# A decoder block's attention values as three float32r products of split operands, with the output sums' in-place multiplications issued directly behind their products

## The chip, the cores and the metric

The kernel runs on one core of a Trainium2 chip. The metric is device time in microseconds (us) of one execution of the whole program, taken several times on the chip; the median is compared. In the profile, PE is the matrix engine, PEld its weight loads, DVE the vector engine, ACT the scalar engine, POOL the GpSimd engine, SP the engine that issues the DMAs. L423 is line 423 of the kernel before.

## The reference, cut to what matters

The program is one decoder layer on x of shape (8, 128, 512): grouped-query attention with 4-bit weights, then cross attention, then a gated low-rank feed-forward, each followed by a layer norm. The change is inside the first part:

```python
q = apply_rope(dequant(x, qw_q)); k = apply_rope(dequant(x, qw_k)); v = dequant(x, qw_v)
scores = einsum('bhqd,bhkd->bhqk', q, k) / sqrt(HD)          # 32 query heads, 8 key heads, HD = 128
attn = softmax(where(causal, scores, min))
ctx = einsum('bhqk,bhkd->bhqd', attn, v)                     # the values product that is changed
x = layernorm(x + dequant_matmul(ctx, qw_o, scales_o))       # its sums over heads are rescaled in place
```

All data is float32. The kernel writes a float32 matrix product in one of two ways: as one matmul on float32 tiles (the trace shows it as two MATMUL records), or as a sum of matmuls on float32r tiles, each operand split into a high part and a low remainder (one record per matmul).

## The kernel before, in words

**Stages.** Up to about 70 us the first weights and inputs are loaded and split. From there to about 505 us runs the attention stage. It has 64 steps: 8 key-head groups g times 8 sequences b. Four steps share one half `hf` of the batch; a half is the unit for which projections are computed. After the steps, a fixed string `ATT_END` (L43) finishes the output sums beside key projections of the cross attention. Cross attention and feed-forward follow and are not touched.

**One step** (L760 to L824) walks the string `SEQUENCE = 'TpOpApOVpOpOp'` (L80). Each letter first calls `tick()`, which advances a slot counter and issues every instruction that was put off until that slot by `later(n, f)` (L242). The order on PE, DVE, ACT and POOL is exactly the order in which the Python code issues (a manual schedule); the order of the DMA issues on SP is left to the scheduler. The letters are:

- `T`, `attention_turn` (L411): four transposes of the softmaxed scores `p` into a PSUM tile `tr`, and a copy on ACT to `pt` (L417).
- `p`: some projection units of a coming half (`group`, L314). A unit is two matmuls (L317) and an evacuation, on ACT for the first of four (L323) and on DVE for the others (L327). After the fourth unit the tile is complete: a query or key tile is then rotated (`rope`, L345: two DMAs that swap halves, then `t`, `sw`, `q` or `k` on POOL, L350 to L352), and a value tile is transposed into `trv` and copied by ACT to `v` (L364).
- `A`, `attention_probs` (L380): scores `sc` of the step two ahead (L384), row minima on DVE (L389), four exponentials on ACT three slots later (L398), then a reciprocal `rden` on DVE (L404) and the normalisation of `p` on POOL (L405).
- `V`, `attention_values` (L420): the product `av` of `v` and `pt` (L423) and its split into `ch` on ACT (L186) and `cl` on DVE (L187).
- `O`, one part of `attention_out` (L442): two matmuls onto a sum `po` (L453) in one of two PSUM banks, `out0` and `out1`, which the parts use in turn. For the first three of four heads the sum is then multiplied in place by a ratio on ACT (L460); the last goes to `accT`, on ACT for g = 0 (L462) and on DVE otherwise (L466). The next part on the same bank waits for that multiplication.

**Delays.** `DELAYS` (L109) gives for each put-off instruction the number of slots, first value while step 0 is issued, second afterwards. `out` is 1 in both, so L460 is issued one letter after its product. There is an entry `pl` of 3 and 2 slots that nothing uses.

**Banks and buffers.** Six PSUM banks (`turn`, L131) rotate over `ps`, `tr`, `trv`, `sc` and `av`: a tile's bank is wanted again by the sixth tile after it. SBUF pool `att` holds `q`, `k`, `v`, `p`, `pt`, `ch`, `cl`, `wo`; pool `proj` holds the projections' tiles and `w0_kv` (L504), low parts of the first weights.

**The last six steps** have no more projections of their own; L777 to L786 open the cross attention's tiles, whose splits (`xwkh`, `ctxh`, `xwvh` on ACT, their low parts on POOL and DVE) run beside them.

Of the kernel before, what the change touches and what calls it, by code (L numbers as in the profile page):

```python
# [10 lines left out]
F32 = mybir.dt.float32  # L11
F32R = mybir.dt.float32r
# [3 lines left out]
ALU = mybir.AluOpType  # L16
# [3 lines left out]
P = 128  # L20
B, S, D = 8, 128, 512
N = B * S
KT = D // P
NH, NKV, HD = 32, 8, 128
REP = NH // NKV
# [10 lines left out]
HALF = 4  # L36
# [51 lines left out]
D_COS = 4  # L88
D_SIN = 10
D_Q = 10  # L90
D_OUT = 1
D_STAT = 3
D_POW = 3
D_APPLY = 8
# [6 lines left out]
S_COS = 3  # L101
S_SIN = 10
S_Q = 10
S_OUT = 1
S_W = 6
S_VT = 6
S_LOAD = 11
# [8 lines left out]
    "q": (S_Q, D_Q),  # L116
    "out": (S_OUT, D_OUT),
    "w": (S_W, D_W),
# [16 lines left out]
def f32(ap):  # L135
    return ap.bitcast(F32)
# [3 lines left out]
def decoder_kernel(ctx: ExitStack, tc: tile.TileContext, a: dict, out: bass.AP):  # L140
    nc = tc.nc
# [7 lines left out]
    def bank(tag, name, shape=(P, 512)):  # L149
        tag = tag if tag in psum["n"] else "turn"  # L150
        return psum["pool"].tile(list(shape), F32, tag=tag, name=name, bufs=psum["n"][tag])

    def pool(name, side="left", bufs=1):
        cm = tc.tile_pool(name=name, bufs=bufs, side=side)
        return cm, cm.__enter__()
# [29 lines left out]
    def split2(hi, lo, src, n=1):  # L185
        nc.scalar.copy(hi, src)  # L186
        later(n, lambda: nc.vector.tensor_tensor(lo, src, f32(hi), ALU.subtract))  # L187
# [49 lines left out]

    delayed, slot, starting, instance = [], [0], [True], {}  # L240

    def later(n, f, projects=False):  # L242

        if slot[0] == 0 or n == 0:
            return f()
        delayed.append((slot[0] + n, f, projects))

    def delay(name):

        return DELAYS[name][0 if starting[0] else 1]  # L250
# [21 lines left out]
    att_cm, att = pool("att")  # L272
    proj_cm, proj = pool("proj", "right")
# [79 lines left out]

        return projection(g, hf, w, j, x[:], rope)

    def values(g, hf, w, v):
        n = f"{g}_{hf}"
        x = proj.tile([P, HN], F32, tag="x", name=f"xv{n}", bufs=3)

        def turn():  # L360
            tr = bank("tr", f"trv{n}", (P, HALF, HD))
            for t in range(HALF):
                nc.tensor.transpose(tr[:, t, :], x[:, ts(t, S)], ident[:])
            nc.scalar.copy(v[:], tr[:])  # L364

        return projection(g, hf, w, REP + 1, x[:], lambda: later(delay("vt"), turn, True))

    def projections(g, hf, w):

        n = f"{g}_{hf}"  # L370
        q = att.tile([P, REP, HN], F32, tag="q", name=f"q{n}", bufs=2)
        k = att.tile([P, HN], F32, tag="k", name=f"k{n}", bufs=2)
        v = att.tile([P, HALF, HD], F32, tag="v", name=f"v{n}", bufs=2)
        units = roped(g, hf, w, REP, k[:], "k")
        for r in (REP - 1, *range(REP - 1)):
            units += roped(g, hf, w, r, q[:, r, :], "q")
        units += values(g, hf, w, v)
        return {"q": q, "k": k, "v": v}, units

    def attention_probs(g, b, t):  # L380
        j, n = b % HALF, f"{g}_{b}"
# [29 lines left out]
    def attention_turn(g, b, p):  # L411
        n = f"{g}_{b}"
        tr = bank("tr", f"tr{n}", (P, REP, S))
        for r in range(REP):
            nc.tensor.transpose(tr[:, r, :], p[:, r, :], ident[:])
        pt = att.tile([P, REP, S], F32, tag="pt", name=f"pt{n}", bufs=2)
        nc.scalar.copy(pt[:], tr[:])  # L417
        return pt

    def attention_values(g, b, t, pt):  # L420
        j, n = b % HALF, f"{g}_{b}"
        av = bank("av", f"av{n}", (P, REP, S))
        nc.tensor.matmul(av[:], t["v"][:, j, :], pt[:], start=True, stop=True)  # L423
        if j == 0:
            for m in "hl":
                t["c" + m] = att.tile([P, REP, HN], F32R, tag="c" + m, name=f"c{m}{n}", bufs=2)
        split2(t["ch"][:, :, ts(j, S)], t["cl"][:, :, ts(j, S)], av[:], delay("cl"))
# [14 lines left out]
    def attention_out(g, hf, t):  # L442

        sums, n = {}, len(OUT_LANES)

        def part(c, r):
            if r == 0:
                sums[c] = bank(OUT_LANES[c % n], f"po{g}_{hf}_{c}")  # L450
            ps = sums[c]
            for i, m in enumerate("hl"):
                nc.tensor.matmul(  # L453
                    ps[:], o_w[g][:, r, ts(c, P)], t["c" + m][:, r, :],
                    start=(r == 0 and i == 0), stop=(i == 1), skip_group_check=True,
                )
            sc = ratios[:, c, g * REP + r : g * REP + r + 1]
            to = accT[:, c, ts(hf, HN)]
            if r < REP - 1:
                later(delay("out"), lambda: nc.scalar.activation(ps[:], ps[:], AF.Copy, scale=sc))  # L460
            elif g == 0:
                later(delay("out"), lambda: nc.scalar.activation(to, ps[:], AF.Copy, scale=sc))  # L462
            else:
                later(
                    delay("out"),
                    lambda: nc.vector.scalar_tensor_tensor(to, ps[:], sc, to, ALU.mult, ALU.add),  # L466
                )

        return [lambda c=c, r=r: part(c, r) for c0 in range(0, KT, n) for r in range(REP) for c in range(c0, c0 + n)]
# [9 lines left out]
    def new_qkv(g):  # L479
        return proj.tile([P, KT, COLS], F32R, tag="w", name=f"w{g}", bufs=2)  # L480

    def new_o(g):
        return att.tile([P, REP, D], F32R, tag="wo", name=f"wo{g}", bufs=2)


    w, wo = new_qkv(0), new_o(0)
# [14 lines left out]


    w0_q = att.tile([P, REP, D], F32R, tag="ch", name="w0_q", bufs=2)
    w0_kv = proj.tile([P, KT, 2 * HD], F32R, name="w0_kv")  # L504

    def w0_low(j):
        return w0_q[:, :, ts(j, HD)] if j < REP else w0_kv[:, :, ts(j - REP, HD)]
# [219 lines left out]
    for i in range(2 * KT):  # L727
        units.pop(0)()
        tick()
        if i in W0_AT:  # L730
            n = W0_AT.index(i) + 2
# [5 lines left out]
    units, more = units + more[:AHEAD], more[AHEAD:]  # L737
    for i, u in enumerate(units, KT):
# [7 lines left out]
        if i in PROBS_AT:  # L746
            b = PROBS_AT.index(i)
# [3 lines left out]
    units = more  # L751
    assert len(units) <= RAMP + WINDOW[3]
    turned, outs = {}, []
    steps = NKV * B

    def at(s):
        g, b = divmod(s, B)
        return g, b, halves[s // HALF]

    for s in range(steps):  # L760
        g, b, t = at(s)
        if s == STARTING:
            starting[0] = False
        w = (s + LEAD) % HALF
        if w == 0:
            h = (s + LEAD) // HALF + 1
            if h < 2 * NKV:
                halves[h], units = half(h)
            else:
                units = []  # L770
        if s == 1:
            scale_ratios()
        if s == B:
            load_small()
# [24 lines left out]
        if b >= HALF and g + 1 < NKV:  # L799
            if b == HALF:  # L800
                o_w[g + 1] = new_o(g + 1)
            load_o(g + 1, o_w[g + 1], b - HALF)

        slots = SEQUENCE.count("p")
        done = 0
        for i, what in enumerate(SEQUENCE):
            tick()
            if what == "p":
                done += 1
                n = len(now) * done // slots - len(now) * (done - 1) // slots  # L810
                start = len(now) * (done - 1) // slots
                for u in now[start : start + n]:
                    u()
            elif what == "T":
                turned[s] = attention_turn(g, b, probs.pop(s))
            elif what == "A":
                if s + LEAD < steps:
                    probs[s + LEAD] = attention_probs(*at(s + LEAD))
            elif what == "V":
                attention_values(g, b, t, turned.pop(s))  # L820
            elif outs:
                outs.pop(0)()
        if b % HALF == HALF - 1:
            outs += attention_out(g, b // HALF, t)  # L824
# [52 lines left out]
    for t in range(B):  # L877
        n = VALUES_FIRST * (t + 1) // B - VALUES_FIRST * t // B
# [7 lines left out]
        tr = transposed(other_bank(f"tr_x1{t}", (P, KT, S)), t)  # L886
        hf, c = t // HALF, ts(t % HALF, S)
# [201 lines left out]
    for hf in range(2):  # L1089
        for m in range(KT):  # L1090
            n = fills.pop(0) if ready else 0
# [548 lines left out]
```

## Time and profile before

| | us |
|---|---|
| median of 3 runs (lowest to highest) | 707.55 (704.76 to 708.47) |
| the profiled execution | 709.09 |
| its span | 707.3 |
| busy in the span: PE / PEld / DVE / ACT / POOL | 653.6 / 486.1 / 498.4 / 487.8 / 461.3 |
| busy from 292 to 350 us (58 us, two halves): PE / DVE / ACT / POOL | 56.78 / 43.72 / 48.81 / 45.97 |
| busy from 467 to 505 us (38 us): PE / DVE / ACT / POOL | 32.40 / 16.11 / 32.11 / 19.14 |

The mean granted PE clock of the execution was 0.976 of full speed. An engine's busy time is the time in which it executed something; PE's records overlap, since the end of a matmul is modelled with the time that its result takes to come out, so PE's busy share is not its load. In a row of groups the columns are: line, engine, operation, tiles (out<-in), shapes, count, then total busy us and mean ns of one, then the engine's idle time just before these instructions and what ended most of it. In a timeline a row is start in us, duration in us, engine, line, operation, tiles, count, and in brackets the idle time before it with what ended it. The chain of waits is followed back from the last instruction, always to what released it; its rows are start, duration, engine, tile, line, count.

### The profile page before, as it was taken

Reading aid. Unit: us, or ns where it says so; the run is one execution under the profiler, and the core shown is the slowest. Engines: PE = TensorE matmul, PEld = TensorE weight load, DVE = VectorE, ACT = ScalarE, POOL = GpSimd, SP = SyncE. Lnnn points to the kernel's source line nnn. Section 1 sums busy time; section 2 is a strip of 40 time slices with the busy share of each in tenths; the row PEclk is TensorE's granted clock in tenths of the full one; section 3 lists DMA queues with packets and bytes.
Section 4 is the critical chain, followed back from the end, with each engine's and each line's share of the span. In section 5 each row is a group of like instructions: output and inputs, shape, how many; then the busy total and the mean of one; then the engine's idle time right before and its main releaser. Section 6 shows DMA issues by size and latency. Waiting matters only on the chain.

```text
span 707.3 us, 11358 instructions
## 1 busy us (share of the span) xinstructions
PE 653.6 (92%) x3476; PEld 486.1 (69%) x3476; DVE 498.4 (70%) x1291; ACT 487.8 (69%) x1211; POOL 461.3 (65%) x450
## 2 busy tenths in 40 slices
PE   6899999999999999999999999978999998479996
PEld 4687678777777767778777777746786765456652
DVE  4869667687777877778777786754366789975465
ACT  3567898987897888888889778888634455323433
POOL 3644977967869678696796977886014367356514
PEclk9999999999999999999999999999999999759998
DMA  8762531532443243244133332244001001100003
GB/s 289 203 183 65 135 98 35 137 97 46 105 120 76 60 135 90 56 117 110 34 85 82 67 102 66 57 164 178 0 1 31 1 1 51 43 1 1 2 0 119
DMA packets 31773, 57.34 MB, mean 81 GB/s; under 512 B 4831, under 2 KB 7135, under 8 KB 31714
## 3 DMA queue, kind: packets, MB, share of 16 engines
q1 hardware_dynamic: 31714, 56.64, 29.4%
q8 instruction: 27, 0.44, 0.3%
q14 instruction: 32, 0.26, 0.1%
HBM read 33.55 MB, written 2.10 MB: 50 GB/s over the span
## 4 chain that ended last, share of the span: by engine, by line
PE 27%; DVE 11%; ACT 7%; POOL 5%; issue 3%; DMA 1%; DVEq 0%; POOLq 0%; SPq 0%; ACTq 0%
PE po L453 4%; PE ps L317 3%; PE pf L1203 3%; PE pxk L692 3%; ACT p L398 3%; PE pxv L656 2%; DVE top L988 2%; PE pxq L692 2%; DVE part L327 2%; POOL sw L351 1%; DVE E L999 1%; PE sc L384 1%; PE pg L1190 1%; ACT po L460 1%; PE av L423 1%
## 5 line engine op out<-in xcount | busy, mean ns | idle before, releaser
L317 PE MATMUL ps<-xh,w 128*128 128x512 f32 x336 | 157.1, 467 | 0.0
L327 DVE SCALAR_TENSOR_TENSOR part<-ps,scales,part 128x512 f32<-128x512 f32 x168 | 125.5, 747 | 32.5 <-ACT part L323 15.0
L317 PE MATMUL ps<-xl,w 128*128 128x512 f32 x336 | 132.3, 394 | 0.0
L460 ACT ACTIVATE po<-po,ratios 128x512 f32<-128x512 f32 x192 | 123.9, 651 | 9.6 <-PE po L453 8.9
L453 PE MATMUL po<-ch,wo 128*128 128x512 f32 x256 | 115.5, 451 | 14.4 <-ACT po L460 13.8
L405 POOL TENSOR_TENSOR p<-p,rden 128x512 f32<-128x512 f32 x64 | 67.2, 1050 | 77.7 <-DVE rden L404 66.3
L398 ACT ACTIVATE p<-p,nmx 128x128 f32<-128x128 f32 x256 | 99.7, 392 | 16.7 <-DVE nmx L389 16.1
L453 PE MATMUL po<-cl,wo 128*128 128x512 f32 x256 | 101.2, 395 | 0.0
L351 POOL TENSOR_TENSOR sw<-sw,tables 128x512 f32<-128x512 f32 x71 | 91.9, 1294 | 13.6 <-DMA sw<-x 12.9
L352 POOL TENSOR_TENSOR q<-t,sw 128x512 f32<-128x512 f32 x62 | 81.5, 1315 | 15.5 <-DVE sw L351 11.1
L350 POOL TENSOR_TENSOR t<-x,tables 128x512 f32<-128x512 f32 x70 | 90.3, 1290 | 0.0
L453 PEld LDWEIGHTS po<-ch,wo 128*128 128x128 f32 x256 | 48.1, 188 | 46.4 <-ACT po L460 30.3
L317 PEld LDWEIGHTS ps<-xh,w 128*128 128x128 f32 x336 | 63.4, 189 | 19.1 <-DVE nmx L389 3.6
L317 PEld LDWEIGHTS ps<-xl,w 128*128 128x128 f32 x336 | 63.5, 189 | 18.6 <-issue 10.1
L389 DVE CUSTOM_DVE_ANT_0 p<-sc,causal 128x128 f32<-128x128 f32 x256 | 58.8, 286 | 23.2 <-PE sc L384 23.2
L384 PEld LDWEIGHTS sc<-k,q 128*128 128x128 f32 x512 | 68.0, 193 | 9.2 <-POOL q L352 2.6
L323 ACT ACTIVATE part<-ps,scales 128x512 f32<-128x512 f32 x84 | 58.0, 691 | 20.8 <-PE ps L317 20.8
L384 PE MATMUL sc<-k,q 128*128 128x128 f32 x512 | 69.4, 278 | 2.8 <-POOL q L352 2.0
L187 DVE TENSOR_TENSOR cl<-av,ch 128x512 fp32r<-128x512 f32 x64 | 44.2, 690 | 34.4 <-ACT ch L186 32.4
L327 DVE SCALAR_TENSOR_TENSOR x<-ps,scales,part 128x512 f32<-128x512 f32 x70 | 52.4, 749 | 21.3 <-PE ps L317 13.4
L423 PE MATMUL av<-pt,v 128*128 128x512 f32 x128 | 65.6, 593 | 0.0
L453 PEld LDWEIGHTS po<-cl,wo 128*128 128x128 f32 x256 | 48.4, 189 | 11.9 <-issue 4.6
(246 smaller groups left out, 1266.7 us busy)
## 6 DMA issues: line engine op xcount, KB each, us to landing
sw<-x SPq DMA_DIRECT2D x160, 128.0 KB, 2.3
raw<-in_qkv SPq DMA_DIRECT2D x28, 384.0 KB, 3.2
oraw<-in_qw_o SPq DMA_DIRECT2D x32, 256.0 KB, 2.8
xraw<-in_xT SPq DMA_DIRECT2D x4, 512.0 KB, 5.9
ctxraw<-in_ctxT SPq DMA_DIRECT2D x2, 1024.0 KB, 5.3
acc<-in_x SPq DMA_DIRECT2D x8, 256.0 KB, 5.6
out<-o SPq DMA_DIRECT2D x8, 256.0 KB, 2.0
xwrawk<-in_WkT SPq DMA_DIRECT2D x1, 1024.0 KB
```

Source lines behind the costliest of these rows:

```text
L317: nc.tensor.matmul(ps[:], w[:, kt, ts(j, HD)], x[:, kt, ts(hf, HN)], start=(i == 0), stop=(i == 1))
L327: nc.vector.scalar_tensor_tensor(to, ps[:], sc, parts[0][:], ALU.mult, ALU.add)
L350: later(delay("cos"), lambda: engine("cos").tensor_tensor(seqs(t[:]), seqs(x[:]), table(cos_t[m]), ALU.mult), True)
L351: later(delay("sin"), lambda: engine("sin").tensor_tensor(seqs(sw[:]), seqs(sw[:]), table(sin_t[m]), ALU.mult), True)
L352: later(delay("q"), lambda: engine("q").tensor_tensor(dst, t[:], sw[:], ALU.add), True)
L384: nc.tensor.matmul(sc[:, r, :], t["q"][:, r, ts(j, S)], t["k"][:, ts(j, S)], start=True, stop=True)
L389: nc.vector.tensor_tensor_reduce(out=p[:, r, :], in0=sc[:, r, :], in1=causal[:], scale=-1.0, scalar=3e38, op0=ALU.add, op1=ALU.min, accum_ ...
L398: nc.scalar.activation(p[:, r, :], p[:, r, :], AF.Exp, scale=-1.0, bias=nmx[:, r : r + 1], accum_out=den[:, r : r + 1],)
L405: nc.gpsimd.tensor_tensor(p[:], p[:], rden[:].unsqueeze(2).to_broadcast([P, REP, S]), ALU.mult)
L423: nc.tensor.matmul(av[:], t["v"][:, j, :], pt[:], start=True, stop=True)
L453: nc.tensor.matmul(ps[:], o_w[g][:, r, ts(c, P)], t["c" + m][:, r, :], start=(r == 0 and i == 0), stop=(i == 1), skip_group_check=True,)
L460: later(delay("out"), lambda: nc.scalar.activation(ps[:], ps[:], AF.Copy, scale=sc))
```

## The change

1. **Values.** The transposed probabilities are no longer copied to one float32 tile `pt` but split: `ph` (float32r) on ACT, and `pl` (float32r) on DVE, two slots later, from `tr` and `ph`. The value tile `v` is split in the same way into `vh` and `vl`, the latter one slot later. The product is three accumulating matmuls, vh by ph, vl by ph, vh by pl.
2. **Output sums.** The delay `out` becomes 0: L460, L462 and L466 are issued directly behind their product. From step 58 on (`ending`), the in-place multiplication is on DVE instead of ACT: 30 of the 192.
3. **Room.** `w0_kv` moves from pool `proj` into one of the two buffers of `cl` in pool `att`.

```diff
-D_OUT = 1
+D_OUT = 0
...
-S_OUT = 1
+S_OUT = 0
...
-            nc.scalar.copy(v[:], tr[:])
+            split2(vh[:], vl[:], tr[:])
...
-        v = att.tile([P, HALF, HD], F32, tag="v", name=f"v{n}", bufs=2)
+        vh = att.tile([P, HALF, HD], F32R, tag="vh", name=f"vh{n}", bufs=2)
+        vl = att.tile([P, HALF, HD], F32R, tag="vl", name=f"vl{n}", bufs=2)
...
-        pt = att.tile([P, REP, S], F32, tag="pt", name=f"pt{n}", bufs=2)
-        nc.scalar.copy(pt[:], tr[:])
-        return pt
-
-    def attention_values(g, b, t, pt):
+        ph = att.tile([P, REP, S], F32R, tag="ph", name=f"ph{n}", bufs=2)
+        pl = att.tile([P, REP, S], F32R, tag="pl", name=f"pl{n}", bufs=1)
+        split2(ph[:], pl[:], tr[:], delay("pl"))
+        return ph, pl
+
+    def attention_values(g, b, t, ph, pl):
         j, n = b % HALF, f"{g}_{b}"
         av = bank("av", f"av{n}", (P, REP, S))
-        nc.tensor.matmul(av[:], t["v"][:, j, :], pt[:], start=True, stop=True)
+        terms = ((t["vh"], ph), (t["vl"], ph), (t["vh"], pl))
+        for i, (v, pt) in enumerate(terms):
+            nc.tensor.matmul(av[:], v[:, j, :], pt[:], start=(i == 0), stop=(i == 2))
...
-            if r < REP - 1:
+            if r < REP - 1 and ending[0]:
+                nc.vector.tensor_scalar(ps[:], ps[:], sc, None, ALU.mult)
+            elif r < REP - 1:
                 later(delay("out"), lambda: nc.scalar.activation(ps[:], ps[:], AF.Copy, scale=sc))
...
-    w0_kv = proj.tile([P, KT, 2 * HD], F32R, name="w0_kv")
+    w0_kv = att.tile([P, KT, 2 * HD], F32R, tag="cl", name="w0_kv", bufs=2)
...
+        if s == steps - 6:
+            ending[0] = True
```

More of the change, by code (lines that the diff above doesn't have):

```diff
@@ L236, in layernorm @@
         return lambda: nc.vector.tensor_scalar(dst, acc[:, t, :], mv[:, 0:1], rstd[:], ALU.subtract, ALU.mult)
-    delayed, slot, starting, instance = [], [0], [True], {}
+    delayed, slot, starting, ending, instance = [], [0], [True], [False], {}
     def later(n, f, projects=False):
@@ L354, in roped, with values @@
         return projection(g, hf, w, j, x[:], rope)
-    def values(g, hf, w, v):
+    def values(g, hf, w, vh, vl):
         n = f"{g}_{hf}"
@@ L376, in projections @@
             units += roped(g, hf, w, r, q[:, r, :], "q")
-        units += values(g, hf, w, v)
-        return {"q": q, "k": k, "v": v}, units
+        units += values(g, hf, w, vh, vl)
+        return {"q": q, "k": k, "vh": vh, "vl": vl}, units
     def attention_probs(g, b, t):
@@ L819, in decoder_kernel @@
             elif what == "V":
-                attention_values(g, b, t, turned.pop(s))
+                attention_values(g, b, t, *turned.pop(s))
             elif outs:
```

## The prediction

> **What bounds the kernel now.** I read the busy times by window first, then the waits, then the chain of waits through one half, then the timelines of POOL, ACT and DVE around a step. From the windows, two of the fourteen halves and the last steps (start:end, span, then PE, PEld, DVE, ACT, POOL busy, clock, DMA share):
>
> ```profile
> 292.00:350.00 58.00, 56.78 (x280) 43.58 (x279) 43.72 (x123) 48.81 (x130) 45.97 (x38) 1.00 0.35 91
> ...
> 467.00:505.00 38.00, 32.40 (x139) 22.57 (x138) 16.11 (x54) 32.11 (x79) 19.14 (x17) 0.96 0.30 111
> ```
>
> In the steady stage PE is nearly always busy and no other engine is far behind: ACT 84%, POOL 79%, DVE 75%. In the last steps PE has 5.6 us of holes and DVE is idle more than half. What PE waits for, from 70 to 490 us:
>
> ```profile
> PE po L453 <- ACT po L460: 13.4, 24, 1.9
> PE sc L384 <- POOL q L352: 2.0, 2, 1.3
> PE po L453 <- DVE accT L466: 0.5, 2, 0.3
> ```
>
> So PE waits almost only for the in-place multiplication on ACT. The chain through one half runs on PE without a break for 12 us, and gives the net price of each PE piece, which the records (592 ns for L423, 394 for L317) do not, since they overlap:
>
> ```profile
> 343.26 0.46 PE po L453 x2
> 343.72 0.86 PE av L423 x2
> 344.58 0.46 PE po L453 x2
> ...
> 505.15 0.70 PE pxk L692 x3
> ```
>
> PE sets the pace, but POOL is a near second. Its timeline in one half (rows left out are as dense):
>
> ```profile
> 348.06 1.04 POOL L405 TENSOR_TENSOR p<-p,rden 128x512 f32<-128x512 f32 x1
> 353.38 1.04 POOL L405 TENSOR_TENSOR p<-p,rden 128x512 f32<-128x512 f32 x1 [4.29 <-DVE rden L404]
> ...
> 360.62 1.04 POOL L405 TENSOR_TENSOR p<-p,rden 128x512 f32<-128x512 f32 x1 [0.58 <-PE ps L317]
> ...
> 375.67 1.29 POOL L352 TENSOR_TENSOR q<-t,sw 128x512 f32<-128x512 f32 x1
> ```
>
> It idles once, until DVE's `rden`, then works 23.6 us to the half's last `q`, done at 376.96. The scores that need it start on PE at 377.86 (third of four there, 0.44 later). In the halves in between, the margin is smaller (348.10 against 348.39).
>
> **Part 1: three passes.** One float32 `av` is 0.86 us net on PE; three float32r products are 0.70 (row x3 above, the same 128x512 form). 0.16 x 64 = 10.2 us less on PE, provided that `ph`, `pl` and `vl` are there in time:
>
> - ACT: `ph` and `vh` are casts for copies. L186 casts the same shape out of PSUM in 580 ns, L417 copies in 592. Nothing.
> - DVE gets 64 `pl` and 16 `vl`, priced by L187, the same form (PSUM minus SBUF): 690 ns. 80 x 0.69 = 55 us, of which the attention stage's DVE idle, 58.0 - 43.7 = 14.3 us per two halves, can take 6.9 per two halves. The order of issue puts them at four places of a half. I walked one half of DVE's timeline (347 to 376) with them inserted: `pl` at 349.2 finds no hole and makes the row minima 0.64 late; `vl` at 352.0 uses the 0.95 us wait before the first `x`, which leaves 0.23; `pl` at 357.4 makes minima 0.58 late, gone by 359.6; `pl` at 364.6 leaves 0.35, gone by 367; `pl` at 371.3 falls into this hole:
>
> ```profile
> 372.29 0.29 DVE L389 CUSTOM_DVE_ANT_0 p<-sc,causal 128x128 f32<-128x128 f32 x1 [1.33 <-PE sc L384]
> ```
>
>  By that walk `pl` is done 0.3 to 1.5 us before the third pass, and the banks of `tr` and `trv`, now held until the subtraction, are free 0.4 to 3.5 us before PE wants them. Hidden, then, if the holes stay; I charge 1 us for lateness that reaches PE.
> - Start: at 54.09 PE wants the second `av`, while DVE works through `scale_ratios` and rope until 56.1 (in the order, `pl` follows the `sw` of 55.41). PE stands some 2.2 us, but 1.3 us later it would have stood 1.36 us before the scores anyway. +1.5 (bounds 0 and 3).
>
> **Part 2: the multiplication one letter earlier.** On PE nothing moves. On ACT and DVE the order shows one steady swap per step: L460 of the `O` before `V` now stands ahead of the four exponentials, not behind:
>
> ```profile
> 307.57 0.40 ACT L398 ACTIVATE p<-p,nmx 128x128 f32<-128x128 f32 x1
> ...
> 309.13 0.63 ACT L460 ACTIVATE po<-po,ratios 128x512 f32<-128x512 f32 x1
> 309.70 0.58 ACT L186 CAST ch<-av 128x512 fp32r<-128x512 f32 x1
> ...
> 311.12 1.21 ACT L460 ACTIVATE po<-po,ratios 128x512 f32<-128x512 f32 x2
> ```
>
> Its product was done at 307.2, so here the multiplication ends 1.6 us sooner, and PE's stall at 309.81 (about 0.66 us net) goes. This pattern comes once a half: 14 x 0.66 = 9.2 at most. But ACT is continuously busy from 307.57 to 314, and PE's next stall (0.63 at 311.81, on the multiplication of 311.12 behind two weight casts) then begins sooner and is longer. I take -2 (bounds -9 and +2). In the other three steps of a half the product ends 0.41 to 0.50 us after the first exponential would start: ACT stands that long with the exponentials queued behind, which come about 1.1 us later; they gate `rden`, and `rden` gates POOL. Before, `rden` started about 0.95 us after the last exponential in the two steps that open POOL's run, so POOL starts about 0.3 us later.
>
> The Trainium skill, "TensorE: Matmul & The Clock Gate", Specifications table at its head, says that ScalarE and VectorE are strict first-in-first-out. That speaks against this swap: nothing passes a waiting multiplication. If all of ACT's waits of 0.45 us in three steps of four came onto the path, it would be 48 x 0.45 = 21.6 us; the rows show ACT idle 9 us per 58, which covers them.
>
> **POOL's give-back.** POOL's margin at a half's boundary is 0.9 + 0.44 or 0.3 + 0.44 us. PE arrives three passes, 0.5 us, sooner, POOL 0.3 later. Every second half then ends short by a few tenths: +3 us over 14 halves (bounds 0 and 7).
>
> **SP.** The order also shows three weight loads (`raw5_0`, `raw6_0`, `raw7_0`) moved ahead of the swap DMAs of one query tile. Each load waits for a cast on ACT: 188.01 follows the cast ending 187.72, and the swap DMAs, before at 186.86, queue behind. 1.3 to 1.5 us later `sw`, on POOL's dense run, minus its margin: 3 x 1.2 = +3.5 us (bounds 0 and 5).
>
> **The end.** From step 58, 30 multiplications leave ACT for DVE. From 462 to 496 us PE waits on L460 thus (weight-load view):
>
> ```profile
> PEld po L453 <- ACT po L460: 8.4, 7, 2.3
> PEld sc L384 <- POOL q L352: 1.5, 1, 1.5
> ```
>
> DVE, 42% busy there, takes them; the form, PSUM to PSUM, is not in the trace. Rows on both sides: 646 ns (L236) and 742 (L466), ACT's own is 651. I take 0.70. Several sit behind `cl` or `pl`, so half of the 8.4 goes: -4 (bounds 0 and -8). After 505 us DVE has room between the output transposes.
>
> The skill's "VectorE: DVE Perf Modes", Specifications, says VectorE sits closer to SBUF and ScalarE closer to PSUM, which speaks against moving a PSUM-to-PSUM operation; L466 against L460 is 91 ns. By the rule's side of the rows, 30 x 0.09 = 2.7 us more DVE time, which is idle time there.
>
> `w0_kv` in `cl`'s buffer: the next tile in that buffer comes at step 4, after the first weights' last use. Nothing; bound 0 to 1.
>
> **Sum.** -10.2 + 1 + 1.5 - 2 + 3 + 3.5 - 4 = -7.2. On the profiled execution 709.09 - 7.2 = 701.9. That execution lies 1.54 above the median of the runs, so for a median 707.55 - 7.2 = **700.3**.
>
> **Rivals.**
> - *POOL becomes the pace.* For: its run is closed in every half. Against: 0.7 to 1.3 us of margin. Then the steady stage gives nothing: AV counts only in 13 steps at the two ends, -2.1, the end -4, the start +1.5, SP +3.5: -1.1, 706.4.
> - *DVE no longer keeps up (slower).* Place: the subtractions in each half, in order, before row minima and `rden`. Five per half are 3.45 us against 7.1 idle. For: DVE's idle consists of in-order waits, and every wait for `ch` (26.2 us from 70 to 490) moves later with the exponentials. Against: the walk finds the holes. It decides from about 0.5 us per half that is not absorbed (14 x 0.5 = 7); at 1.25, 17.5 - 7.2 = +10.3: 718.
> - *The passes do not cost a third of 0.70 each* because the third waits for `pl` in every step: 0.3 us would be 64 x 0.3 = 19, +12: 719. Against: 0.3 us or more to spare everywhere but the start.
>
> **How the numbers follow.** Forecast case (692 to 704) 0.52; POOL 0.21; DVE 0.19; waiting passes 0.08. A difference of 0.5%, 3.5 us, is about what a measurement of this kernel can tell from no change. The forecast is faster (0.51) but for 0.01, POOL's case is 0.07 faster, 0.12 same, 0.02 slower, the other two are slower but for 0.03 within the bound: faster 0.58, same 0.15, slower 0.27. The low bound takes the better ends of the end and of part 2: 690. Leaving out the upper half of the slower cases gives 716.
>
> **What would show it.** Right: net 0.70 for an `av` in the chain; hardly any PE wait on `pl` after 70 us; in 467 to 505 fewer PE waits on `po`; halves some 0.2 us shorter than now (29.2 us from one `av` to that four steps later). POOL's case: PE `sc` waiting for POOL `q` in each half. DVE's: PE `ps` or `av` waiting for DVE. Wrong at the root: an `av` that is not cheaper, or ACT's idle gone.

## The result, and the profile after

| | before | after |
|---|---|---|
| median (lowest to highest), us | 707.55 (704.76 to 708.49) | 711.57 (710.44 to 713.51) |
| the profiled execution / its span, us | 709.09 / 707.3 | 711.19 / 709.3 |
| busy in the span: PE / DVE / ACT / POOL, us | 653.6 / 498.4 / 487.8 / 461.3 | 644.7 / 564.3 / 469.7 / 462.1 |

The ratio of after to before is 1.0065, 95% interval 1.0051 to 1.0080: 4.6 us slower on 707, where the forecast was 7.2 faster. PE's busy time did fall, DVE's rose by 66. In the kernel after, `rden` is L405, the normalisation of `p` L406, `av` L427, the product onto `po` L457, its multiplication L464 on DVE and L466 on ACT, `accT` L472. The windows of after, with the columns as before (start:end, span, then PE, PEld, DVE, ACT, POOL busy, clock, DMA share, GB/s):

```profile
292.00:350.00 58.00, 54.21 (x281) 44.58 (x282) 48.32 (x132) 47.66 (x128) 44.56 (x38) 1.00 0.36 92
467.00:505.00 38.00, 30.79 (x140) 23.71 (x139) 31.45 (x79) 21.88 (x62) 21.90 (x19) 0.91 0.33 121
```

In the steady stage PE has now 3.8 us of holes per 58 where it had 1.2, and no engine has taken its place: DVE is at 83%, ACT at 82%, POOL at 77%. With holes on every engine, no single one sets the pace; that points to a chain of waits that runs over several of them. In the last steps the work has gone from ACT to DVE, and PE is no denser (the clock column there is 0.91, for 0.96 before). What PE waits for, from 70 to 490 us (total, times, longest):

```profile
PE sc L385 <- POOL q L352: 10.6, 11, 1.9
PE po L457 <- ACT po L466: 10.2, 13, 1.5
...
PE po L457 <- DVE po L464: 3.6, 4, 1.6
...
PE av L427 <- DVE pl L187: 0.3, 1, 0.3
```

The waits for ACT's multiplication are fewer (13 for 24), those for the query tiles five times as long in total, and DVE's own multiplications have made a new wait. The three products cost what was forecast. PE's timeline, from the first product of an `av` to the instruction behind it, 0.69 us net, with nothing idle between (the other two products are left out):

```profile
346.49 0.39 PE L427 MATMUL av<-ph,vh 128*128 128x512 f32 x1
...
347.18 0.39 PE L457 MATMUL po<-ch,wo 128*128 128x512 f32 x1
```

POOL's timeline in one half: its run opens at 357.09, has a hole of 1.83 us before the second `p`, and ends with the last `q` at 381.42; PE has started the scores that need that `q` at 380.89 and stands in them (1.30 us, where they take 1.05 elsewhere):

```profile
357.09 1.04 POOL L406 TENSOR_TENSOR p<-p,rden 128x512 f32<-128x512 f32 x1 [3.76 <-PE po L457]
...
365.20 1.04 POOL L406 TENSOR_TENSOR p<-p,rden 128x512 f32<-128x512 f32 x1 [1.83 <-DVE rden L405]
...
380.13 1.29 POOL L352 TENSOR_TENSOR q<-t,sw 128x512 f32<-128x512 f32 x1
```

DVE's timeline ahead of that second `p` shows where its reciprocal `rden` was (the four accumulator reads and three more row minima are left out). From 360.61 to 364.89 DVE has no hole; `pl` is one of the things queued ahead:

```profile
360.61 0.75 DVE L327 SCALAR_TENSOR_TENSOR x<-ps,scales,part 128x512 f32<-128x512 f32 x1 [0.19 <-DVE part L327]
361.27 0.68 DVE L187 TENSOR_TENSOR pl<-tr,ph 128x512 fp32r<-128x512 f32 x1
361.87 0.28 DVE L390 CUSTOM_DVE_ANT_0 p<-sc,causal 128x128 f32<-128x128 f32 x1
...
362.71 1.60 DVE L327 SCALAR_TENSOR_TENSOR part<-ps,scales,part 128x512 f32<-128x512 f32 x2
364.23 0.74 DVE L472 SCALAR_TENSOR_TENSOR accT<-po,ratios,accT 128x512 f32<-128x512 f32 x1
364.89 0.17 DVE L405 RECIPROCAL rden<-den 128x4 f32<-128x4 f32 x1
```

### The profile page after: what moved, and what is told of

It is laid out like the page before. It is cut to its first block, busy times and chain, and to the rows that moved or that the text cites. A ratio compares the mean times of both kernels' runs of the same rounds, so it can differ in the third digit from the quotient of the medians.

```text
span 709.3 us, 11607 instructions
## 1 busy us (share of the span) xinstructions
PE 644.7 (91%) x3540; PEld 503.2 (71%) x3540; DVE 564.3 (80%) x1401; ACT 469.7 (66%) x1181; POOL 462.1 (65%) x450
## 4 chain that ended last, share of the span: by engine, by line
PE 31%; POOL 15%; DVE 14%; ACT 5%; issue 4%; DMA 2%; POOLq 0%; SPq 0%; DVEq 0%; ACTq 0%
PE po L457 5%; PE ps L317 5%; POOL sw L351 5%; POOL q L352 4%; POOL t L350 3%; PE pf L1211 3%; PE pxk L698 3%; PE sc L385 2%; DMA sw<-x 2%; POOL p L406 2%; PE pxv L662 2%; DVE part L327 2%; DVE top L996 2%; PE pxq L698 2%; ACT p L399 1%
## 5 line engine op out<-in xcount | busy, mean ns | idle before, releaser
L317 PE MATMUL ps<-xh,w 128*128 128x512 f32 x336 | 141.2, 420 | 0.0
L406 POOL TENSOR_TENSOR p<-p,rden 128x512 f32<-128x512 f32 x64 | 67.2, 1050 | 87.4 <-PE po L457 49.7
L466 ACT ACTIVATE po<-po,ratios 128x512 f32<-128x512 f32 x162 | 105.5, 657 | 21.4 <-PE po L457 20.6
L457 PE MATMUL po<-ch,wo 128*128 128x512 f32 x256 | 105.0, 410 | 15.4 <-ACT po L466 10.2
L457 PE MATMUL po<-cl,wo 128*128 128x512 f32 x256 | 101.3, 396 | 0.0
L385 PE MATMUL sc<-k,q 128*128 128x128 f32 x512 | 71.6, 279 | 10.6 <-POOL q L352 10.6
L457 PEld LDWEIGHTS po<-ch,wo 128*128 128x128 f32 x256 | 48.4, 189 | 32.3 <-ACT po L466 13.6
L317 PEld LDWEIGHTS ps<-xl,w 128*128 128x128 f32 x336 | 63.9, 190 | 10.2
L457 PEld LDWEIGHTS po<-cl,wo 128*128 128x128 f32 x256 | 48.6, 190 | 9.5
L399 ACT ACTIVATION_READ_ACCUMULATOR p<-p,nmx 128x1 f32 x256 | 48.3, 189 | 0.0
```

What stands on the lines that cost most here:

```text
L317: nc.tensor.matmul(ps[:], w[:, kt, ts(j, HD)], x[:, kt, ts(hf, HN)], start=(i == 0), stop=(i == 1))
L385: nc.tensor.matmul(sc[:, r, :], t["q"][:, r, ts(j, S)], t["k"][:, ts(j, S)], start=True, stop=True)
L399: nc.scalar.activation(p[:, r, :], p[:, r, :], AF.Exp, scale=-1.0, bias=nmx[:, r : r + 1], accum_out=den[:, r : r + 1],)
L406: nc.gpsimd.tensor_tensor(p[:], p[:], rden[:].unsqueeze(2).to_broadcast([P, REP, S]), ALU.mult)
L457: nc.tensor.matmul(ps[:], o_w[g][:, r, ts(c, P)], t["c" + m][:, r, :], start=(r == 0 and i == 0), stop=(i == 1), skip_group_check=True,)
```

## The experiments

Each was timed in five rounds against the kernel before on the same chip; changes in us are the ratio's, on 707.

| kernel | median, us | ratio to before | 95% interval |
|---|---|---|---|
| early multiplication alone (e2) | 701.03 | 0.9915 | 0.9897 to 0.9933 |
| last six steps on DVE alone (e3) | 706.40 | 0.9989 | 0.9974 to 1.0005 |
| split alone (e1) | 720.66 | 1.0190 | 1.0169 to 1.0212 |
| split and last six steps (e4) | 720.62 | 1.0191 | 1.0170 to 1.0213 |
| e2 + subtractions, unread (e5) | 704.87 | 0.9972 | 0.9956 to 0.9988 |
| e2 + three products, no subtractions (e6) | 697.67 | 0.9871 | 0.9845 to 0.9897 |
| e2 + one product, no subtractions (e8) | 700.39 | 0.9907 | 0.9882 to 0.9931 |
| e2 + three products + subtractions, unread (e10) | 707.50 | 1.0011 | 0.9993 to 1.0028 |
| e10 with `pl` behind the row minima (e17) | 706.84 | 1.0003 | 0.9988 to 1.0019 |
| after without the last six steps' change (e9) | 708.56 | 1.0026 | 1.0007 to 1.0044 |
| e9 with `pl` behind the row minima (e7) | 718.56 | 1.0164 | 1.0131 to 1.0197 |
| e7 with the products one letter later (e18) | 711.94 | 1.0069 | 1.0047 to 1.0091 |
| e9, normalisation 7 slots behind (e13) | 707.40 | 1.0002 | 0.9986 to 1.0017 |
| e9, normalisation 9 slots behind (e15) | 712.83 | 1.0070 | 1.0049 to 1.0092 |
| e2, normalisation 7 slots behind (e14) | 700.97 | 0.9912 | 0.9890 to 0.9934 |
| e2 + last six steps on DVE (e16) | 703.78 | 0.9950 | 0.9931 to 0.9970 |
| late multiplication, three products, no subtractions (e12) | 706.47 | 0.9988 | 0.9970 to 1.0007 |
| e2, last `q` of a half on DVE (e11) | 729.06 | 1.0316 | 1.0287 to 1.0344 |

Part of what is left between kernels goes with the granted clock. Beside e1, the kernel before took 705.3 us at a mean clock of 0.983 and 709.4 at 0.975, about 0.4 us per 0.001 over its 17 executions. By that slope (an estimate) the clock is worth under 1 us in most comparisons below. It is worth more in e8 (mean 0.968, for 0.979 in e6), and about 1 us in e5 (0.981, for 0.978 in e2), in e12 (0.977, for 0.979 in the kernel before beside it) and in the kernel after (0.975, for 0.977 in e9).

### First theory: the early multiplication did it

In the trace of after, the multiplication stands ahead of the exponentials and waits for its product, in the step that opens POOL's run the exponentials come 2 us later behind their scores than before, and the run opens 1.1 to 1.25 us later. So the first theory was that this swap is the loss and the split the gain. The parts of the change one by one:

```diff
# e1, from after: the split alone (with w0_kv's move), without the last six steps' change
# e4: the same, with the last six steps' change
-D_OUT = 0
+D_OUT = 1
-S_OUT = 0
+S_OUT = 1
# e2, from before: the early multiplication alone
-D_OUT = 1
+D_OUT = 0
-S_OUT = 1
+S_OUT = 0
# e3, from before: the last six steps' multiplications alone, as in the change
```

> The kernel before with the three float32r products and their subtractions alone; the output sums stay one letter behind their product, and all on ACT. Theory (the earlier multiplication holds the exponentials back, so the reciprocal that opens POOL's run of rotations comes 1.25 us late and POOL sets the pace): without it the run opens at most 0.3 us later, PE keeps most of the 10.2 us, 699 to 702 us. Rival D (the subtractions make row minima and the first rotated tile late on DVE, and that alone delays POOL's run): the time stays at 708 to 712 us and scores still wait for POOL's q in most halves.

> The kernel before with both delays of the output sums at 0 and nothing else. Theory: the exponentials come 0.65 to 1.1 us later, POOL's run opens later, 709 to 714 us, with scores waiting for POOL's q. Rival D: POOL's margin of 0.7 to 1.3 us covers it, and a stall of PE per half goes, 702 to 707 us.

> The kernel before with only the 30 multiplications from step 58 on put on DVE, directly behind their products. Both theories: the steady stage is unchanged; by the prediction 4 us less, 703 to 704 us. If the last steps are paced by something else (the transposes' normalised probabilities on POOL, DVE's own queue), 706 to 709 us.

> The changed kernel with both delays of the output sums back at 1. Theory: 695 to 701 us, clearly faster than the kernel before. Rival D: 707 to 711 us, within 2 us of the changed kernel's 711.6.

The theory falls: e2 is 6.0 us faster than before, e1 13.4 slower. The exponentials did come later in e2 too, but what the swap takes from PE is worth more. Waits of e2 from 70 to 490, weight-load view (the waits of PEld, which overlap PE's work and so come out longer than PE's own); before, the first line was 29.5 us in 42 waits:

```profile
PEld po L453 <- ACT po L460: 11.5, 11, 1.9
...
PEld sc L384 <- POOL q L352: 7.6, 9, 2.2
```

The price is the second line (2.3 in 2 waits before): POOL has used up its margin. The last six steps' change gives -0.8 (e3, not told from zero) and, beside the split, nothing (e4). With the late multiplication the split fails by another path. From 70 to 490 in e1, ACT's exponentials wait 27.5 us for the row minima (11.9 before), and the multiplication, issued behind them, passes that on to PE:

```profile
PEld po L457 <- ACT po L466: 51.5, 63, 2.1
```

### The split taken apart, with the multiplication early

```diff
# e5 to e8 are without the last six steps' change
# e5: the float32 product stays; subtractions done, nothing reads them (vh is float32 too)
-        ph = att.tile([P, REP, S], F32R, tag="ph", name=f"ph{n}", bufs=2)
+        ph = att.tile([P, REP, S], F32, tag="ph", name=f"ph{n}", bufs=2)
-        for i, (v, pt) in enumerate(terms):
-            nc.tensor.matmul(av[:], v[:, j, :], pt[:], start=(i == 0), stop=(i == 2))
+        nc.tensor.matmul(av[:], t["vh"][:, j, :], ph[:], start=True, stop=True)
# e6: three products (vh,ph three times), no subtractions; vh likewise, vl = vh
# e8: as e6, the first product only
-        split2(ph[:], pl[:], tr[:], delay("pl"))
-        return ph, pl
+        nc.scalar.copy(ph[:], tr[:])
+        return ph, ph
# e7: as after but for this delay and the last six steps
-D_PL = 2
+D_PL = 5
```

> The kernel after, without the last six steps' multiplications on DVE, whose product is again one float32 matmul of float32 tiles; all 64 pl and 16 vl subtractions are still done on DVE, but nothing reads them. PE works as before, DVE as after. Base for comparison: the kernel before with the earlier multiplication alone, 701.0. Theory Q (a subtraction costs by its place in DVE's queue, ahead of the row minima and the evacuations, whose lateness goes through the exponentials to ACT's multiplication and to POOL): at least the whole loss of the kernel after against that base shows, 708 to 720. Theory W (the cost is the third product waiting for pl): nothing reads pl here, so 700 to 704. Theory P (POOL or another engine is the pace and the split by itself costs nothing): 700 to 703.

> Three float32r products as in the kernel after, without the subtractions: the second product reads vh and the third reads ph again, so the low parts are left out of the computation (and the sum is three times the high product). Without the last six steps' multiplications on DVE. PE works as after, DVE as before. Base 701.0 as above. Theory Q: PE's saving of 10.2 us is real and only the subtractions take it back: 690 to 696. Theory W: the same, 690 to 696. Theory P: with the multiplication early, POOL already sets the pace (in the base PE waits 13 us for query tiles), so most of PE's 10 us is given back: 698 to 702.

> The kernel after, without the last six steps' multiplications on DVE, with the delay of pl at 5 slots instead of 2 after step 0: the subtraction is issued behind the row minima of the step, ahead of nothing that the exponentials need; the third product then has two letters less to wait for it. Theory Q: the minima and exponentials are on time again; against 711.6 of the kernel after the gain is 4 to 10, less what the third product now waits: 702 to 708. Theory W: the third product waits about 0.5 us longer per step, 64 times: 715 to 740. Theory P: within 2 of the kernel after, 710 to 713.

> One float32r product of ph and vh alone, no second and third product, no subtractions: the low parts are left out of the computation. Without the last six steps' multiplications on DVE. PE has 40 us less than the base of 701.0 (0.63 less for each of 64). It measures how far a faster PE can take the stage before another engine stops it. Theories Q and W say nothing of it beyond 661 if nothing else binds. Theory P: POOL's run of 23.6 us a half behind a wait for rden is the pace: 693 to 700.

Against e2, e5 is 4.0 us slower and e6 3.1 faster (the intervals of e6 and e2 touch). So the saving on PE is worth a third of its 10.2 us, and e8 shows why: one product instead of three takes another 29 us from PE (64 x 0.46) and is no faster than e6. Two things hold e8 back besides: 2.5 us of waits that SP's order makes, told below, and the lower clock, some 4 us by the slope above. Without both, by this estimate, it would be about 4 us faster than e6, for 29 us of work. PE's waits from 70 to 490 have grown instead, from 10.2 and 9.4 in e6:

```profile
PE po L454 <- ACT po L463: 23.9, 17, 2.2
...
PE sc L385 <- POOL q L352: 16.2, 12, 2.6
```

With the multiplication early, PE's work does not set the pace. e7 is the rival with the waiting third product, made real: PE waits for `pl` 56 times in the weight-load view, 47.0 us, and the time is 718.6. In the kernel after that view has 6.7 us.

```profile
PEld av L427 <- DVE pl L187: 47.0, 56, 1.4
```

### What the parts give together

By their medians, e2, e5 and e6 would add to 701.5. The next four close the sum and test POOL as the pace.

```diff
# e9, from after
-        if s == steps - 6:
-            ending[0] = True
# e10: e9 with
-        terms = ((t["vh"], ph), (t["vl"], ph), (t["vh"], pl))
+        terms = ((t["vh"], ph), (t["vh"], ph), (t["vh"], ph))
# e11: e2 with the last q of a half on DVE
+        then = "v" if name == "q" and n % (REP + 1) == REP else THEN_ON[name]
# e12: e6 with
-D_OUT = 0
+D_OUT = 1
-S_OUT = 0
+S_OUT = 1
```

> The kernel after with the last six steps' 30 multiplications on ACT again, as before; three passes and the earlier multiplication stay. It closes the sum: the earlier multiplication alone 701.0, with the subtractions unread 704.9, with the three passes but no subtractions 697.7; if these add, 701.5, while the kernel after is at 711.6. Theory A (adds up; the last six steps' change is what costs the rest): 701 to 704. Theory B (the rest is an interaction of passes and subtractions, and the last six steps' change is worth nothing, as in the two comparisons with the late multiplication): 709 to 712.

> As the run without the last six steps' change, but all three products read vh and ph: both subtractions are still done on DVE, and nothing waits for them; the low parts are left out of the computation. Theory B1 (the interaction is PE standing in its own queue for pl at the third product, at step 0 and in the steady steps, with everything behind it): 700 to 704, the sum of the parts. Theory B2 (PE's earlier arrival is worth nothing while DVE is late, because POOL's run sets the half; the wait for pl only takes time that PE would stand anyway): within 2 of the run without the last six steps' change, 707 to 712. In between, the start alone: 3 to 4 below that run.

> The kernel before with the earlier multiplication alone (701.0), and in every half the last rotated query tile's sum q on DVE instead of POOL: POOL's run is one operation (1.13 us net) shorter per half and its end some 0.5 us earlier. Theory P (POOL's run from rden to the last q is the pace once the multiplication is early): PE's waits for the query tiles, 8.5 us in the trace, go for the most part, 693 to 698. Rival (the sum on DVE waits for POOL's sw in DVE's queue, with row minima and evacuations behind it): 701 to 710.

> Three float32r products without the subtractions (the second reads vh, the third ph again; the low parts are left out of the computation), with the multiplication one letter later as in the kernel before, so POOL has its margin of about 1.3 us a half. The split with its subtractions was 720.6 here, the kernel before 707. Theory Q (with the late multiplication the subtractions' lateness on DVE goes through the exponentials to the multiplication and to PE; PE's saving of 10 is real): 696 to 700. Theory P (PE's saving is worth little, since another engine stops PE): 702 to 707. Were the three passes themselves what costs (weight loads, banks): 712 or more.

The sum closes in steps: early multiplication -6.0 (e2), three products -3.1 (e6), subtractions +9.9 (e10), reading them +1.1 (e9, not told from zero by the intervals), the last six steps +2.8 (after): +4.7, measured 4.6. Theory A is wrong, and so is most of B1: PE's wait for `pl` is at most about 1 of the 10. The subtractions cost 9.9 beside three products and 4.0 in e5 (about 5 at e2's clock), where PE's product is float32. The traces say in which part of the kernel: the 53 steps from the `av` of step 4 to that of step 57 take 387.3 us in before, 382.8 in e2, 381.4 in e6, 389.9 in e10, 389.5 in e9 and 389.3 in after. So 8.5 us of the 9.9 are in the steady stage, where reading `pl` and `vl` adds nothing; and after's loss on e9 is not there but behind step 57.

Where the 9.9 sits is read from POOL's runs, first `p` to last `q`, added up over the 14 halves from g = 1 on: 333.1 us in e2, 333.4 in e6, 338.6 in e5, 341.2 in e10, 341.8 in e9, 342.4 in after. Of the 7.8 between e6 and e10, 4.0 are the hole before the second `p` and 3.5 are waits for `sw`; of these, 2.7 come in just the three halves in which the order of DMA issues on SP puts a weight load ahead of the swap DMAs. That reordering is the scheduler's; it is there in after, e8, e9, e10, e13, e15 and e17, and not in e1, e2, e5, e6, e7, e12, e14, e16 and e18, so the two runs from which the sum of 701.5 was made did not have it. In after the three waits are these, at 192.68, 252.03 and 311.76 us in POOL's timeline, the first of them:

```profile
192.68 1.29 POOL L351 TENSOR_TENSOR sw<-sw,tables 128x512 f32<-128x512 f32 x1 [1.13 <-DMA sw<-x]
```

SP's order was not tried alone: that the three waits are due to it is argued from order and timeline.

e12 answers what PE's saving is worth without POOL in the way: 0.8 us, not told from zero. Two halves take 58.3 us from scores to scores, in before and in e12 alike. What PE saved at `av` it waits at `po`:

```profile
PEld po L456 <- ACT po L465: 41.8, 66, 2.1
```

That is 12.3 us more than in before (in PE's own view 18.0 for 13.4). `V` stands between the scores and the last `O` of a step; that `O` waits for a multiplication that is behind the exponentials, and these are timed by the scores. Whatever gets shorter in between only makes the wait longer. Against e12, e1 has the subtractions in addition and is 14.3 us slower.

e11 is a miss of theory P's hope, and its rival was far too mild: the sum `q` on DVE waits for POOL's `sw` in DVE's queue, with everything behind it, +28 us over e2. (One `q` on POOL is 1.25 us from start to start, not 1.13 as expected.)

```profile
DVE q L353 <- POOL sw L352: 45.5, 14, 4.5
```

### POOL's order, and the last six steps

```diff
# e13, from e9, and e14, from e2
-D_NORM = 6
+D_NORM = 7
# e15, from e9
+D_NORM = 9
# e16: e3 with D_OUT = 0, S_OUT = 0
```

> The kernel after without the last six steps' change (708.6), and the normalisation of p one slot later (7 slots behind the scores instead of 6), so that in POOL's run the second p stands behind sw and q of the first query tile instead of ahead of them. Theory P (with the early multiplication POOL's run is the pace of the stage; its only hole is the one ahead of the second p, 1.2 us with no subtractions and 1.5 to 1.7 with them; the subtractions cost by making this hole and one sw later): the hole is filled, 14 times 1.2 to 1.7: up to 17 to 24 less until PE's own waits bind, 690 to 699. Rival (the subtractions' lateness comes through exponentials and row minima, whatever POOL does first): 705 to 710.

> The kernel before with the early multiplication (701.0) and the same later normalisation. Theory P: the hole of 1.2 us a half is filled, PE's waits for query tiles (8.5 us) go, PE with its float32 product binds again: 692 to 697. If then the kernel with three passes and the later normalisation is faster than this one, the split pays once POOL is out of the way; by the size of PE's saving it would be up to 10 faster, with the subtractions' lateness less. Rival: 700 to 702.

> As the first kernel of this call, with the normalisation at 9 slots: the first p of POOL's run then also stands behind the first t, which waits for the key tile's x on DVE (0.3 us earlier than rden in the trace). Theory P: another 0.3 us per half or nothing, 688 to 699, unless the p that the transposes read comes too late (it has some 4 us). Rival: 705 to 710.

> The kernel before with the early multiplication and the last six steps' multiplications on DVE, without the split. Alone with the late multiplication that change was worth -0.5; with split and early multiplication it cost 3. Theory E1 (it costs where ACT's multiplication is early already: on DVE the multiplication stands in a queue with row minima and evacuations, and PE waits for it): 702 to 705. Theory E2 (it costs only beside the subtractions, which fill DVE's queue): 700 to 701.5.

The hole before the second `p` was filled in e13 and e14, but the times hardly moved: e13 is 1.7 us under e9, e14 equal to e2. The edit moved the first `p` as well: its `rden` now stands behind `cl`, and the run opens about 1 us later (medians behind the scores of its half: 7.2 for 6.2 in e13, 6.8 for 5.6 in e14). So the run's end, the last `q`, stayed within 0.3 us of where it was: 30.2 behind the first scores of its half for 30.4 in e13, 29.8 for 29.5 in e14 (medians). That the times stayed too fits POOL's run as the pace; but it isn't the separate test that was meant. e15 opens the run 4 us later and is 3.1 us slower than e9.

e16 answers for the last six steps: +2.5 us on e2, by itself, without the subtractions (E1). Its interval still touches that of e2; after and e9 lie apart (+2.8), though there about 1 us goes with the clock, which is at half from 479.1 to 485.9 us in the trace of after and only from 474.9 to 478.3 in e9's. In the trace of after, from 440 to 535 us, the two forms of the multiplication:

```profile
L464 DVE TENSOR_SCALAR po<-po,ratios 128x512 f32<-128x512 f32 x30 | 22.2, 748 | 1.7 <-PE po L457 1.5
...
L466 ACT ACTIVATE po<-po,ratios 128x512 f32<-128x512 f32 x11 | 7.2, 660 | 2.0 <-PE po L457 2.0
```

DVE takes 88 ns longer, 2.6 us over the 30. From 440 to 530 us PE's weight loads wait 8.7 us for DVE's `po` in e16, in 10 waits, and 4.6 for ACT's in e2, in 4. In 10 waits the longer operation is 0.9 us; most of the loss is then DVE's queue, by the waits, which no run tested apart. The rule of the Trainium skill cited in the prediction, "VectorE: DVE Perf Modes", Specifications, that ScalarE sits closer to PSUM, agrees in sign with the 88 ns. The page "Perfetto Trace Analysis", section "Optimizing Scalar/DVE Operations", gives some 125 ns of access overhead per instruction for DVE on PSUM and 51 for ScalarE. It calls these engine-busy times and puts the profiled latency at about twice that; by an estimate from its figures the difference would be 74 to 148 ns, and the measured 88 lies in between.

### Which of DVE's late results

```diff
# e17: e10 with                       # e18: e9 with both
-D_PL = 2
+D_PL = 5
-SEQUENCE = 'TpOpApOVpOpOp'
+SEQUENCE = 'TpOpApOpVOpOp'
```

(e17 has only the first of the two edits.)

> As the run whose products read only vh and ph while both subtractions are still done (707.5), with pl issued on DVE at 5 slots, behind the row minima instead of ahead of them; nothing waits for pl or vl, and the low parts are left out of the computation. DVE does exactly the same work in another order. Theory M (the subtractions cost because the row minima queue behind them, and exponentials, rden and POOL's run behind these): back to the run without subtractions, 697 to 702. Theory L (they cost as load, because the evacuations of rotated tiles and rden come late wherever the subtraction stands): 705 to 709.

> The kernel after without the last six steps' change (708.6), pl behind the row minima as above, and the values' three products one letter later (behind a projection unit), so that PE waits less for pl; everything is read, nothing is left out. With pl behind the minima and the products at their old place PE waited 42 us for it and the time was 718.6; one unit is 0.46 us net, twice that in two steps of four. Theory M: the exponentials are on time and most of that wait goes, 698 to 706. Theory L: 708 to 714, with part of the wait left.

Theory M falls: with `pl` behind the row minima e17 is within 0.6 us of e10. `pl` then stands behind the minima but still ahead of `rden`. DVE's timeline in e17, three minima and their reads left out:

```profile
328.82 0.75 DVE L327 SCALAR_TENSOR_TENSOR x<-ps,scales,part 128x512 f32<-128x512 f32 x1 [0.19 <-PE sc L385]
...
330.33 0.69 DVE L187 TENSOR_TENSOR pl<-tr,ph 128x512 fp32r<-128x512 f32 x1
330.93 1.60 DVE L327 SCALAR_TENSOR_TENSOR part<-ps,scales,part 128x512 f32<-128x512 f32 x2
332.45 0.74 DVE L472 SCALAR_TENSOR_TENSOR accT<-po,ratios,accT 128x512 f32<-128x512 f32 x1
333.11 0.17 DVE L405 RECIPROCAL rden<-den 128x4 f32<-128x4 f32 x1
```

It is 4.29 us from `x` to `rden`, as in after (4.28). Without the subtraction, e6 has the same chain in 3.68:

```profile
294.17 0.75 DVE L327 SCALAR_TENSOR_TENSOR x<-ps,scales,part 128x512 f32<-128x512 f32 x1 [0.19 <-DVE part L327]
...
297.19 0.74 DVE L471 SCALAR_TENSOR_TENSOR accT<-po,ratios,accT 128x512 f32<-128x512 f32 x1
297.85 0.17 DVE L405 RECIPROCAL rden<-den 128x4 f32<-128x4 f32 x1
```

So theory L: what counts, by these timelines, is that a subtraction stands between the last hole and `rden`, not on which side of the minima. No run of its own tested this. In e6 this `rden` follows the last exponential by 0.53 to 0.66 us in most halves, in e10 by 1.07: the 0.4 to 0.5 us are the larger hole in POOL's run. e18 shows the other side: in the step that opens POOL's run the exponentials start 3.0 us behind their scores (median; 4.2 in e9), SP's order is the old one, PE hardly waits for query tiles, and its weight loads wait 38.9 us for `pl`; the time is 3.0 us above e9's. No place that was tried suits both.

## Why the prediction was wrong, step by step

**The sign was wrong: faster was forecast, slower came.** The nearest account was split over two rivals: POOL as the pace (706.4) and DVE not keeping up (718, place "before row minima and `rden`", price from 0.5 us per half). Both happened, at 711.6.

| step | on record | measured |
|---|---|---|
| three products on PE | -10.2 | -3.1 (e6 on e2); -0.8 with the late multiplication (e12) |
| subtractions on DVE | +1 | +9.9 with SP's part (e10 on e6) |
| SP's loads ahead of swap DMAs | +3.5 | 3.5 of waits in the three halves of after, by the timeline; in the line above |
| start, third product waiting | +1.5 | +1.1 (e9 on e10), not told from zero |
| earlier multiplication, with POOL's give-back | -2 + 3 | -6.0 (e2) |
| the last six steps | -4 | +2.8 (after on e9); +2.5 (e16 on e2) |

- **The step that failed first is "0.16 x 64 = 10.2 us less on PE".** The price 0.70 was right. That PE's busy time counts whole was taken from "PE sets the pace", read off a busy share of 98%. But almost the only waits that PE had, on ACT's multiplication, stood behind `av` in the same step and took the saving up: two halves took 58.3 us in before and in e12 alike. e12 and e8 show it from both sides.
- **The second is the walk along DVE.** It found lateness "gone by 359.6". It was made on the order of before, where `accT` follows `rden`. Part 2 of the same change issues L466 one letter earlier too, ahead of `rden`, into the place that the walk had left for lateness to vanish in. The prediction spoke of L460's swap only. The walk also asked whether `pl` was in time for PE, which it was (1 us), and not what came late behind it. The hole ahead of POOL's second `p`, 0.58 us in a row that the prediction shows while its text has POOL idle only once, is 1.83 in after.
- **The third is the last six steps.** DVE's multiplication was sized at 0.70 us, measured 0.75; the gain was taken from ACT's queue with the late multiplication. With the early one, ACT's queue was already cured, and only DVE's was left to wait in. With the late one it was worth -0.8 (e3), not -4, and not told from zero.
- **The earlier multiplication had the right mechanism and the wrong size.** PE's waits for it went as the first bound said (9.2 at most); the charge for ACT's next stall was too careful, and POOL's give-back is in the -6.0. POOL's run was to open 0.3 us later; it opened 5.6 us behind its scores in e2 and 6.2 in after, for 5.0 in before.
- **SP was right in place, and its waits in size**; what they cost in time was not tried alone. At the start PE waits for `pl` as long as forecast, 2.2 us, but the net cost of that is not told from zero. `w0_kv`'s move was not tried alone; e6 has it and is faster than e2. PE's timeline in after:

```profile
55.56 0.56 PE L427 MATMUL av<-pl,vh 128*128 128x512 f32 x1 [2.22 <-DVE pl L187]
```

- The Trainium skill's rule that VectorE and ScalarE are strict first-in-first-out ("TensorE: Matmul & The Clock Gate", the table at its head) was weighed against ACT, where it cost little. Its weight was on DVE: a `rden` of 0.17 us behind a subtraction of 0.69, in 14 halves.

The fastest kernel here with all of the computation is e2, the early multiplication alone: 701.03, or 0.85% under before and 1.5% under after; e14 is equal. What stays open: SP's part by a run of its own, and whether the split would pay with `rden` ahead of `pl`. That was not tried: in the present sequence the letter `V`, which reads `pl`, issues the exponentials that this `rden` needs.

## What to carry to other kernels

Before a saving on the busiest engine is counted, look for that engine's next wait behind the saved piece: if it waits for a chain that started ahead of the piece, the saving becomes wait. Work put on an engine "with idle time" is priced by the small operations queued behind it that another engine is waiting for, and each must be looked up in the new order, with all the other edits of the change in place. Parts of a change should be added only with their interaction in mind: here -6 (e2), -3 (e6) and +4 (e5) became +1 (e10).

## What the runs showed of the hardware that was not expected

The multiplication in place out of PSUM took 748 ns on DVE and 660 on ACT for 128x512. Otherwise the rows were as forecast: three float32r products 0.69 us net for 0.86 of a float32 one, a subtraction 0.68 us.
